# Two-layer graph attention on one Trainium2 core: twelve edge tiles of each layer read row by row from SyncE, with the rows' places in registers

## The chip, the core and the metric

The kernel runs on one core of a Trainium2 chip. The time is the device time of one execution in microseconds (us). Before the change it is 2088.41 us, the median of 3 runs (2086.89 to 2090.06).

## What is computed

The reference normalises `x` (6250 nodes of 768 numbers), runs two graph attention layers over 100,000 edges sorted by destination, and a small network per node, and adds the result to `x`. Cut to what matters:

```python
h = jnp.maximum(_layernorm(x, axis=-1), 0.0)
h = relu(gat_conv(h, src, dst, W1, a_src1, a_dst1, b1, heads=4))      # 256 wide
h = relu(gat_conv(h, src, dst, W2, a_src2, a_dst2, b2, heads=1))
out = x + relu(h @ Wm1 + bm1) @ Wm2 + bm2

def gat_conv(x, src, dst, W, a_src, a_dst, bias, heads):
    h = (x @ W).reshape(n, heads, -1)
    e = leaky_relu(alpha_s[src] + alpha_d[dst], 0.2)     # then a softmax over the edges of each dst
    out = segment_sum(h[src] * alpha[:, :, None], dst)
```

So each layer needs, for every edge, the row `h[src]` of a table in HBM, with a few numbers on the scores of that source beside it.

## The kernel before, in words

**Tiles.** 128 edges make a tile; 782 tiles hold the 100,000 edges. Two tiles make a pair (one buffer `G` of 128 x 2 rows), two pairs a group `g`, and there are 196 groups (`NG`) in each layer. 128 nodes make a node tile; there are 49 (`NT`).

**Stages.** First the features of layer 1 are computed node tile by node tile, kept in SBUF (`kept`), and written to `table[1]` (`store1`, L541). Then `layer_edges` (L688) runs over the groups for layer 1, and again for layer 2. While layer 1 runs, each finished node tile is turned into a row block of `table[2]` (`Node1.steps`, L1051 to L1079). In layer 2 each finished node tile goes through the small network to the output (`Node2.steps`, L1164).

**Gathering.** `gather(g)` (L705) reads the rows of group `g`: for each tile one indirect DMA issued by GpSimd (L722), which reads the 128 rows that 128 indices name. It is called up to 8 groups ahead of use (`AHEAD`, L945). The buffers `G` come in turn from a pool of 20 (L280). Some pairs are fetched in another way: 27 pairs of layer 1 (`SOON`) were gathered during the first stage, stored in HBM (`soon_d`), and come back by one ordinary DMA of SyncE (L324); rows that did not exist yet are filled in by matmuls with a mask (L350). Ten pairs of layer 2 (`NEXT`) are treated likewise (L380, L391). So GpSimd issues 728 tiles of layer 1 and 762 of layer 2 at L722.

**Use.** `pair(g, p)` (L791) takes a pair: VectorE forms the weights of its edges (L800 to L813), TensorE adds the weighted rows by destination (L824). `pair(g, 0)` and `pair(g, 1)` stand at two places of the loop over groups (L937 to L1005).

**SyncE.** It does no arithmetic here. It issues, in the order of the program, all ordinary DMAs: in layer 1 the loads `drow` (L679) from which VectorE makes the masks, the stores of the masks `mask_d` (L741), the `soon` loads (L324, L330), and the stores to `table[2]` (L1078); in layer 2 the loads of the masks (L686), of `x` (L1143), and the stores of the output (L1223). The DMAs take eight semaphores in turn, and each DMA waits until the one eight before it has landed, so at most eight are in flight. A DMA whose data are not made yet holds up what stands behind it on SyncE.

The numbers of a table row: 256 features, the ones for the softmax's sums, and the powers of the scores, 268 in layer 1 and 259 in layer 2 (`TW`, L176).

Of the kernel before, what the change touches and what calls it, by code (L numbers as in the profile page):

```python
# [10 lines left out]
F32 = mybir.dt.float32  # L11
BF16 = mybir.dt.bfloat16
I32 = mybir.dt.int32
AF = mybir.ActivationFunctionType
ALU = mybir.AluOpType
AX = mybir.AxisListType

P = 128
# [3 lines left out]
HID = 256  # L22
# [34 lines left out]
NEXT_GROUP = [16 * i + 11 for i in range(len(NEXT))]  # L57
NEXT_AT = {2 * g + 1: i for i, g in enumerate(NEXT_GROUP)}
NEXT_FROM = min(NEXT)


def portions(there):
# [30 lines left out]
def kernel(  # L93
# [79 lines left out]
    heads = {1: 4, 2: 1}  # L173

    RW = {1: 4 * (HID // 4 + 1), 2: HID + 2}
    TW = {1: RW[1] + 8, 2: RW[2] + 1}  # L176
    table, sd = {}, {}
    for layer, H in heads.items():
        table[layer] = dram.tile([NT * P, TW[layer]], F32, name=f"table{layer}")
# [48 lines left out]
    def powers(e1, e2, s):  # L228

        nc.scalar.activation(e1, s, AF.Exp)  # L230
        nc.scalar.activation(e2, s, AF.Exp, scale=SLOPE)
# [4 lines left out]
    def edge_places(ones):  # L236

        dst_i = ones.tile([P, NET], I32, name="dst_i")
        dri = ones.tile([NCH, CH], I32, name="dri")
        nc.sync.dma_start(src_i, src_cols)  # L240
        yield
        yield
        soonest = sorted(range(len(SOON)), key=SOON.__getitem__)
        for i in range(0, len(SOON), 2):
            for k in soonest[i:i + 2]:
                soon_places(k)
            yield
        for to, of in ((dst_i, dst_cols), (dri, dst_rows)):
            nc.sync.dma_start(to, of)
            yield  # L250
            yield
        for layer in bT:
            with nc.allow_non_contiguous_dma(reason="256 numbers"):
                nc.sync.dma_start(bT[layer], {1: b1, 2: b2}[layer].rearrange("(k p) -> p k", p=P))
            yield
        b = ones.tile([P, OUT_DIM // P], F32, name="b")
        with nc.allow_non_contiguous_dma(reason="768 numbers"):
            nc.sync.dma_start(b, bm2.rearrange("(p k) -> p k", p=P))
        yield

        drm = ones.tile([NCH, CH], BF16, name="drm")
        nc.scalar.activation(dst_f, dst_i, AF.Copy)
        yield
        for d, to in ((dst_i, dcol), (dri, drm)):
            nc.vector.tensor_scalar(d, d, PAD_DST | P - 1, None, ALU.bitwise_and)
            yield
            nc.scalar.activation(to, d, AF.Copy)
            yield
        nc.sync.dma_start(dmod_d, drm)
        bp = ones.tile([P, 3, OUT_DIM // P], BF16, name="bp")  # L270
        rest = ones.tile([P, 2, OUT_DIM // P], F32, name="brest")
        in_parts(nc.vector, [bp[:, k] for k in range(3)], b, rest[:, 0], rest[:, 1])
        yield
        with nc.allow_non_contiguous_dma(reason="768 numbers"):
            nc.sync.dma_start(bm2_d.rearrange("s (p k) -> p s k", p=P), bp)
# [1 line left out]


    bT = {layer: const.tile([P, KH], F32, name=f"bT{layer}") for layer in (1, 2)}
    gp = edges_stack.enter_context(tc.tile_pool(name="gathered", bufs=2 * (AHEAD + 2)))  # L280
    rowsp = edges_stack.enter_context(tc.tile_pool(name="rows", bufs=3))
    maskp = edges_stack.enter_context(tc.tile_pool(name="masks", bufs=6))

# [73 lines left out]
    def soon_whole(G, k):  # L357
        i, t = divmod(k, 2)
        row = G[soon_pair[i]][:, t]
        nc.vector.scalar_tensor_tensor(row, row, soon_ok[:, i, t:t + 1], soon_m.pop(k),  # L360
                                       ALU.mult, ALU.add)

    next_i = const.tile([P, len(NEXT), 2], I32, name="next_i")
    next_ok = const.tile([P, len(NEXT), 2], F32, name="next_ok")
# [80 lines left out]
    with tc.tile_pool(name="w1p", bufs=1) as wp, tc.tile_pool(name="x1", bufs=6) as xp, \  # L445
# [72 lines left out]
        def keep1(i, h_ps, rstd):  # L518
            row = kept[i]
            nc.scalar.activation(heads_row(row)[:, :, :HID // 4],  # L520
                                 h_ps[:, :HID].rearrange("p (h c) -> p h c", h=4), AF.Copy, scale=rstd)
            if i >= BARE:
                nc.scalar.activation(sd[1][:, i], h_ps[:, HID:], AF.Copy, scale=rstd)
                powers(row[:, RW[1]:RW[1] + 4], row[:, RW[1] + 4:], sd[1][:, i, :4])

        def halve(of):

# [8 lines left out]

        def scores1(i):
            nc.vector.tensor_reduce(sd[1][:, i], halves.pop(i), AX.X, ALU.add)
            powers(kept[i][:, RW[1]:RW[1] + 4], kept[i][:, RW[1] + 4:], sd[1][:, i, :4])

        def store1(i):  # L541
            nc.sync.dma_start(table[1][i * P:(i + 1) * P], kept[i])
# [1 line left out]
        halves = {}  # L544
        for row in kept:
            nc.gpsimd.memset(heads_row(row)[:, :, HID // 4:], 1.0)
        warm_ps = ps.tile([P, 4 * P], F32, name="warm_ps", tag="o", bufs=3)

        def warm(n):
# [138 lines left out]
    def layer_edges(layer, H, node, pre, matched, pre_pool):  # L688
# [4 lines left out]
        with tc.tile_pool(name=f"eg{layer}", bufs=6) as eg, \  # L693
# [11 lines left out]
            def gather(g):  # L705
                if not 0 <= g < NG:
                    return
                for t in tiles(g):
                    k = TPG * g + t
                    soon = k // 2 in (SOON_AT if layer == 1 else NEXT_AT)  # L710
                    if k // 2 not in G:
                        skip = int(g >= SHORT and k // 2 % (4 if g < SHORT + 7 else 2 if g < SHORT + 14 else 1) == 0)
                        skip += g >= SHORT + 21
                        G[k // 2] = (soon_back(SOON_AT[k // 2], skip) if soon and layer == 1 else
                                     next_back(NEXT_AT[k // 2], skip) if soon else
                                     rows_in(layer, skip))
                    if soon:
                        continue
                    n = min(P, LEAD + E - k * P)
                    if n < P:  # L720
                        nc.vector.memset(G[k // 2][:, k % 2], 0.0)
                    nc.gpsimd.indirect_dma_start(  # L722
                        out=G[k // 2][:n, k % 2], out_offset=None, in_=table[layer],
                        in_offset=bass.IndirectOffsetOnAxis(ap=src_i[:n, k:k + 1], axis=0))
# [66 lines left out]
            def pair(g, p):  # L791

                if 2 * p not in tiles(g):
                    return
                Gp = G.pop(TPG // 2 * g + p)
                e1, e2 = ((Gp[:, :, RW[1]:RW[1] + 4], Gp[:, :, RW[1] + 4:]) if layer == 1 else
                          (Gp[:, :, HID:HID + 1], Gp[:, :, HID + 2:]))
                at = TPG * (g % 4) + 2 * p
                v = w = e_ps[g // 4][:, at:at + 2]
                nc.vector.tensor_mul(v, e2, v)  # L800
                if layer == 2:
                    w = sm.tile([P, 2, H], F32, name="w")
                    nc.vector.tensor_max(w, v, e1)  # L803
                    hw = hwp.tile([P, 2, P], F32, name="hw")
                    for t in range(2):
                        k = TPG * g + 2 * p + t
                        nc.vector.tensor_scalar(hw[:, t], iota_ps, dcol[:, k:k + 1], w[:, t],  # L807
                                                ALU.is_equal, ALU.mult)
                else:
                    nc.vector.tensor_max(w, v, e1)  # L810
                    hw = hwp.tile([P, 2, H, C + 1], F32, name="hw")
                    nc.vector.tensor_mul(  # L812
                        hw, Gp[:, :, :RW[1]].rearrange("p t (h c) -> p t h c", h=H),  # L813
                        w.unsqueeze(3).to_broadcast([P, 2, H, C + 1]))
                u = g // 2
                if u not in o_ps:
                    o_ps[u] = ps.tile([P, RW[layer]], F32, name="o_ps", tag="o", bufs=3)
                for t in range(2):
                    k = 2 * p + t
                    if layer == 2:  # L820
                        l, r = hw[:, t], Gp[:, t]
                    else:
                        l, r = hot[g][:, k], hw[:, t].rearrange("p h c -> p (h c)")
                    nc.tensor.matmul(o_ps[u], l, r[:, :RW[layer]], start=(g % 2 == 0 and k == 0),  # L824
                                     stop=(g % 2 == 1 and k == tiles(g)[-1]))
# [111 lines left out]
            for g in range(NG):  # L937
# [7 lines left out]
                while gathered < min(NG, g + 1 + min(AHEAD, max(4, SHORT - g), max(2, SHORT + 19 - g))):  # L945
                    gather(gathered)
                    gathered += 1
                pair(g, 0)
                if g == NG - 1:
                    pair(g, 1)  # L950
# [42 lines left out]
                    next_steps(g, pre_pool, sm, G)  # L993
                if layer == 1 and 100 <= g < 100 + len(NEXT):
                    next_places(g - 100)
                if g < NG - 1:
                    pair(g, 1)
                advance(g, 1)
# [29 lines left out]
    with tc.tile_pool(name="w2p", bufs=1) as wp, tc.tile_pool(name="wk2", bufs=2) as wk:  # L1028
# [4 lines left out]
        class Node1:  # L1033
# [17 lines left out]
            def steps(self, t, sum_, most=None, last=None):  # L1051
# [21 lines left out]
                renewed.add(t)  # L1073
                row = kept[t][:, :TW[2]]
                nc.scalar.activation(row[:, :HID], h_ps[:, :HID], AF.Copy)
                powers(row[:, HID:HID + 1], row[:, HID + 2:], h_ps[:, HID:HID + 1])
                nc.vector.memset(row[:, HID + 1:HID + 2], 1.0)
                nc.sync.dma_start(table[2][t * P:(t + 1) * P], row)  # L1078
                nc.scalar.activation(sd[2][:, t], h_ps[:, HID:], AF.Copy)  # L1079
# [459 lines left out]
```

## Time and profile before

| what | value |
|---|---|
| median of 3 runs | 2088.41 us |
| the profiled execution's own time | 2088.15 us |
| its span in the profile | 2086.1 us |
| GpSimd (POOL) busy | 1528.1 us, 73% |
| TensorE (PE) busy | 1730.2 us, 83% |
| VectorE (DVE) busy | 1472.2 us, 71% |
| first and last indirect DMA of L722 begin at | 167.43 us, 2065.66 us |
| layer 1: first pair, and first pair of group 188, begin at | 175.56 us, 1056.02 us |
| layer 2: the same two | 1120.07 us, 2036.07 us |

A line of the profile such as `L722 POOL DMA_INDIRECT G<-table,src_i` is a group of instructions: the line of the kernel, the engine, the operation, what is written from what. `SPq` is the queue of SyncE: the time that it takes to issue a DMA is shown in the order of time, but not counted as busy. Idle time is put down to what ended it ("issue" is time in which an engine waits for nothing that the profile shows). The views used are the page (groups of instructions with their sums), the timeline, the windows (busy time of each engine in a stretch), the view of one source line, the list of DMA issues, and the chain of work that ended last.

### The profile page before, as it was taken

The page shows a single profiled execution, that of the slowest core. Times are in us where ns is not written, and L with a number is a line of the kernel's source. Part 1 is how long each engine was busy: PE and PEld are TensorE (multiplying, and loading weights), DVE is VectorE, ACT ScalarE, POOL GpSimd, SP SyncE. Part 2 cuts the span into 40 slices and gives each one's busy share as a digit, 9 for nine tenths or more (in the row PEclk, how much of TensorE's full clock was granted, in tenths as well). Part 3 has the DMA queues.
Part 4 walks back from the last instruction along what each step waited for, and adds up shares of the span by engine and source line. Part 5 has one row for each costly group of instructions (what it writes and reads, how often), then busy time and mean ns, then how long its engine had stood idle before and what let it go on. Part 6 is the DMA issues. An engine that isn't in the chain of part 4 may idle for free.

```text
span 2086.1 us, 28258 instructions
## 1 busy us (share of the span) xinstructions
PE 1730.2 (83%) x8323; PEld 1292.4 (62%) x8325; DVE 1472.2 (71%) x4315; ACT 449.3 (22%) x1409; POOL 1528.1 (73%) x1666
## 2 busy tenths in 40 slices
PE   9995989999999899888774887787787787787877
PEld 6883768778777687666542555555555555555544
DVE  7756888998989899888873655665565565565554
ACT  5761111111111121111120111111111111111111
POOL 7167777777777777777777777777777777777774
PEclk9997999999999999998996899989998998988889
DMA  9999666666666666666649466556556556555553
GB/s 346 294 336 336 183 174 186 189 191 186 178 184 191 188 184 176 188 191 184 168 124 270 125 184 191 166 181 189 169 178 189 172 174 190 171 176 181 170 178 113
DMA packets 173752, 403.78 MB, mean 194 GB/s; under 512 B 37063, under 2 KB 61470, under 8 KB 173590
## 3 DMA queue, kind: packets, MB, share of 16 engines
q0 software_dynamic: 75040, 210.90, 37.9%
q1 hardware_dynamic: 97180, 189.49, 26.0%
q10 hardware_dynamic: 1370, 1.48, 0.3%
q8 instruction: 70, 1.15, 0.2%
q14 instruction: 92, 0.75, 0.1%
HBM read 333.42 MB, written 68.31 MB: 193 GB/s over the span
## 4 chain that ended last, share of the span: by engine, by line
PE 28%; DMA 25%; DVE 22%; issue 13%; POOL 9%; DVEq 0%; ACT 0%; SPq 0%; POOLq 0%; ACTq 0%
DMA G<-table,src_i 22%; PE o_ps L824 11%; POOL G L722 8%; PE y_ps L1194 5%; DVE hw L812 5%; PE h_ps L515 4%; PE missing L350 4%; DVE hot L750 3%; DVE soon_hit L337 3%; DVE iota_ps L800 2%; DVE iota_ps L810 2%; DVE hw L807 2%; DVE mask L739 1%; DMA xt<-in_x 1%; DMA xTt<-in_xT 1%
## 5 line engine op out<-in xcount | busy, mean ns | idle before, releaser
L722 POOL DMA_INDIRECT G<-table,src_i x1490 | 1420.4, 953 | 454.0 <-issue 319.3
L824 PE MATMUL o_ps<-G,hw 128*128 128x258 f32 x1564 | 457.6, 427 | 206.5 <-DVE hw L807 204.8
L824 PE MATMUL o_ps<-hw,hot 128*128 128x260 f32 x1564 | 427.9, 412 | 112.2 <-DVE hw L812 108.6
L824 PEld LDWEIGHTS o_ps<-G,hw 128*128 128x128 f32 x1564 | 305.2, 208 | 332.9 <-DVE hw L807 273.9
L800 DVE TENSOR_TENSOR iota_ps<-G,iota_ps 128x8 f32<-128x8 f32 (+1 forms) x782 | 130.2, 166 | 442.1 <-DMA G<-table,src_i 431.4
L824 PEld LDWEIGHTS o_ps<-hw,hot 128*128 128x128 f32 x1564 | 300.3, 200 | 206.4 <-DVE hw L812 152.1
L844 ACT ACTIVATE sum<-acc 32x260 f32<-32x260 f32 (+1 forms) x384 | 160.0, 417 | 1133.5 <-DVE acc L835 1069.8
L350 PE MATMUL missing<-kept,soon_hit 128*128 128x268 f32 x1396 | 339.0, 394 | 0.0
L807 DVE TENSOR_SCALAR hw<-iota_ps,dcol,w 128x128 f32<-128x128 f32 x782 | 285.0, 406 | 14.5
L812 DVE TENSOR_TENSOR hw<-G,iota_ps 128x520 f32<-128x520 f32 x391 | 272.0, 696 | 30.2 <-DVE iota_ps L810 1.4
L350 PEld LDWEIGHTS missing<-kept,soon_hit 128*128 128x128 f32 x1396 | 263.2, 192 | 46.3
L1194 PE MATMUL y_ps<-wm,mT 128*128 128x384 f32 x392 | 189.4, 615 | 0.0
L515 PE MATMUL h_ps<-w,r 128*128 128x264 f32 (+1 forms) x588 | 137.1, 386 | 2.5 <-ACT r L505 2.5
L750 DVE TENSOR_TENSOR hot<-iota_ps,dcol 128x512 f32<-128x512 f32 x196 | 133.7, 682 | 0.0
L515 PEld LDWEIGHTS h_ps<-w,r 128*128 128x128 f32 x588 | 108.3, 191 | 22.0 <-ACT r L505 3.5
L1194 PEld LDWEIGHTS y_ps<-wm,mT 128*128 128x128 f32 x392 | 80.8, 228 | 57.3 <-issue 32.6
L337 DVE TENSOR_TENSOR soon_hit<-soon_of,iota_ps 128x768 f32<-128x768 int32 (+6 forms) x110 | 109.1, 992 | 0.2
L313 POOL DMA_INDIRECT G<-table,soon_i x54 | 51.4, 952 | 69.3 <-DVE cent L474 42.5
L835 DVE SCALAR_TENSOR_TENSOR acc<-acc,keep,o_ps 128x260 f32<-128x260 f32 (+1 forms) x192 | 91.4, 476 | 0.9 <-PE o_ps L824 0.9
L810 DVE TENSOR_TENSOR iota_ps<-iota_ps,G 128x8 f32<-128x8 f32 x391 | 68.2, 174 | 13.5 <-DVE iota_ps L800 0.2
L803 DVE TENSOR_TENSOR w<-iota_ps,G 128x2 f32<-128x2 f32 x391 | 62.5, 160 | 13.3
L1024 ACT ACTIVATE rT<-tp,bT 128x128 f32<-128x128 f32 x196 | 61.3, 364 | 32.9 <-PE tp L1018 31.4
(424 smaller groups left out, 1324.0 us busy)
## 6 DMA issues: line engine op xcount, KB each, us to landing
xt<-in_x SPq DMA_DIRECT2D x96, 384.0 KB
drow<-dmod_d SPq DMA_DIRECT2D x49, 512.0 KB
mask_d<-mask SPq DMA_DIRECT2D x97, 256.0 KB
mask<-mask_d SPq DMA_DIRECT2D x97, 256.0 KB
G<-table,src_i POOLq DMA_INDIRECT x1490
out<-y SPq DMA_DIRECT2D x48, 384.0 KB
xTt<-in_xT SPq DMA_DIRECT2D x36, 384.0 KB
soon_d<-G SPq DMA_DIRECT2D x27, 268.0 KB
```

The source lines that it names most:

```text
L337: nc.vector.tensor_tensor(soon_hit[k, part][:, :b - a], soon_of[i][:, t * P:(t + 1) * P].unsqueeze(1).to_broadcast([P, b - a, P]), nid_ps[ ...
L350: nc.tensor.matmul(soon_p[k], hit[:, T - a], kept[T], start=(T == there), stop=(T == NT - 1))
L515: nc.tensor.matmul(h_ps[:, :n], r[:, k], w1[:, k, :n], start=(k == 0), stop=(k == KI - 1))
L722: nc.gpsimd.indirect_dma_start(out=G[k // 2][:n, k % 2], out_offset=None, in_=table[layer], in_offset=bass.IndirectOffsetOnAxis(ap=src_i[: ...
L750: nc.vector.tensor_tensor(hot[g][:, T[0]:T[0] + n], iota_ps.unsqueeze(1).to_broadcast([P, n, P]), dcol[:, k:k + n].unsqueeze(2).to_broadca ...
L800: nc.vector.tensor_mul(v, e2, v)
L807: nc.vector.tensor_scalar(hw[:, t], iota_ps, dcol[:, k:k + 1], w[:, t], ALU.is_equal, ALU.mult)
L810: nc.vector.tensor_max(w, v, e1)
L812: nc.vector.tensor_mul(hw, Gp[:, :, :RW[1]].rearrange("p t (h c) -> p t h c", h=H), w.unsqueeze(3).to_broadcast([P, 2, H, C + 1]))
L824: nc.tensor.matmul(o_ps[u], l, r[:, :RW[layer]], start=(g % 2 == 0 and k == 0), stop=(g % 2 == 1 and k == tiles(g)[-1]))
L844: nc.scalar.activation(done[t][r], acc[r], AF.Copy)
L1194: nc.tensor.matmul(y_ps, mT[:, j], wm2[:, j, s * half:(s + 1) * half], start=False, stop=(j == KH - 1))
```

## The change

Six pairs of each layer, the first pairs of groups 33, 64, 95, 126, 157 and 188 (`EACH_GROUP`), are no longer gathered by GpSimd. Their 256 rows each are read by 256 DMAs of SyncE, each of one row. In the loop over groups, a new function `each_rows` stands ahead of each `pair`: in each of the 32 groups that end two ahead of the pair's own, SyncE first loads eight places from SBUF into eight registers with one instruction, then issues four row DMAs, and four more ahead of the group's second pair. For each row a register instruction multiplies the place by four (numbers to bytes). The windows of the six pairs follow on each other and overlap by one group, so that SyncE issues eight rows in every group from 0 to 186 and sixteen in five of them: 192 sets of eight, 1,536 rows, in each layer. The places (source index times row length) are worked out once by VectorE from a copy of the sources (`each_src`, six small DMAs in the first stage).

The rows of the tables become 269 and 263 numbers long (one and four unused numbers more); a memset of one number in each of the 49 `kept` tiles fills the gap of layer 1. The pool of `G` has 18 buffers in place of 20; the six pairs lie in a pool `each` of two buffers.

```diff
+EACH_GROUP = [33 + 31 * i for i in range(6)]
+EACH = len(EACH_GROUP)
+EACH_AT = {2 * g: i for i, g in enumerate(EACH_GROUP)}
+EACH_SLOTS = 32
+EACH_ROWS = 2 * P // EACH_SLOTS
...
-    TW = {1: RW[1] + 8, 2: RW[2] + 1}
+    TW = {1: RW[1] + 9, 2: RW[2] + 5}
...
-    gp = edges_stack.enter_context(tc.tile_pool(name="gathered", bufs=2 * (AHEAD + 2)))
+    gp = edges_stack.enter_context(tc.tile_pool(name="gathered", bufs=2 * (AHEAD + 1)))
...
+    def each_sources(pool):
+
+        each_src = pool.tile([2 * EACH, P], I32, name="each_src")
+        rows = src_rows.rearrange("k (t p) -> (k t) p", t=2)
+        for i, g in enumerate(EACH_GROUP):
+            nc.sync.dma_start(each_src[2 * i:2 * i + 2], rows[4 * g:4 * g + 2])
+        return each_src
+
+    def each_places(each_src):
+
+        for layer in heads:
+            nc.vector.tensor_scalar(each_at[layer], each_src, float(TW[layer]), None, ALU.mult)
+
+    def each_rows(layer, g, half):
+
+        W, n = TW[layer], EACH_ROWS
+        for i, at in enumerate(EACH_GROUP):
+            s = g - (at - 1 - EACH_SLOTS)
+            if not 0 <= s < EACH_SLOTS:
+                continue
+            if half == 0:
+                if s == 0:
+                    each_G[i] = eachp.tile([P, 2, max(TW.values())], F32, name="each_G")[:, :, :W]
+                regs = [nc.sync.alloc_register(f"each_{layer}_{i}_{s}_{j}") for j in range(n)]
+                nc.sync.load(regs, each_at[layer][2 * i + s * n // P:2 * i + s * n // P + 1, s * n % P:s * n % P + n])
+                each_regs[i] = regs
+            flat = table[layer].rearrange("n w -> (n w)").unsqueeze(0)
+            for j in range(half * (n // 2), (half + 1) * (n // 2)):
+                t, p = divmod(s * n + j, P)
+                place = nc.sync.snap(each_regs[i][j], donate=True, min_val=0, max_val=(NT * P - 1) * W)
+                nc.sync.dma_start(each_G[i][p:p + 1, t], flat[:, ds(place, W)])
...
+            nc.gpsimd.memset(row[:, RW[1] + 8:], 0.0)
...
+                    if k // 2 in EACH_AT:
+                        if k % 2 == 0:
+                            G[k // 2] = each_G[EACH_AT[k // 2]]
+                        continue
...
+                each_rows(layer, g, 0)
                 pair(g, 0)
...
+                each_rows(layer, g, 1)
                 if g < NG - 1:
                     pair(g, 1)
```

The first piece of SyncE's program shown is that of layer 1 about the store of node tile 1 (`kept_116`) to `table[2]` (`table_99`), before the change; `table_97` below is `table[1]`:

```order
L1078 DMA table_99<-kept_116 128x259
L741 DMA mask_d<-mask 128x1024
L324 DMA G<-soon_d 128x536
L679 DMA drow<-dmod_d 128x2048
L741 DMA mask_d<-mask 128x1024
```

The same place after the change, with rows that only repeat left out:

```order
L1128 DMA table_99<-kept_116 128x263
L789 DMA mask_d<-mask 128x1024
L404 REGISTER_ALU
L404 DMA each_G<-table_97 1x269
...
L331 DMA G<-soon_d 128x538
L398 TENSOR_LOAD each_at_168
L404 REGISTER_ALU
L404 DMA each_G<-table_97 1x269
...
L723 DMA drow<-dmod_d 128x2048
```

Between the two old neighbours on SyncE there now stand four or eight row DMAs, each with its register instruction, and the load of eight registers once a group.

GpSimd's program from the first stage's early gathers to the end of layer 2, before the change:

```order
L313 DMA G<-table_97,soon_i 128x268 x54
L722 DMA G<-table_97,src_i 128x268 x727
L722 DMA G<-table_97,src_i 32x268
L380 DMA G<-table_99,next_i 128x259 x20
L722 DMA G<-table_99,src_i 128x259 x128
L1152 TENSOR_LOAD bad_i
L722 DMA G<-table_99,src_i 128x259 x633
L722 DMA G<-table_99,src_i 32x259
```

And after it:

```order
L320 DMA G<-table_97,soon_i 128x269 x54
L770 DMA G<-table_97,src_i 128x269 x715
L770 DMA G<-table_97,src_i 32x269
L423 DMA G<-table_99,next_i 128x263 x20
L770 DMA G<-table_99,src_i 128x263 x128
L1202 TENSOR_LOAD bad_i
L770 DMA G<-table_99,src_i 128x263 x621
L770 DMA G<-table_99,src_i 32x263
```

Twelve indirect DMAs of each layer are gone; the order of the others is as it was.

More of the change, by code (lines that the diff above doesn't have):

```diff
@@ L240, in edge_places @@
         nc.sync.dma_start(src_i, src_cols)
+        each_src = each_sources(ones)
         yield
         yield
+        each_places(each_src)
         soonest = sorted(range(len(SOON)), key=SOON.__getitem__)
@@ L361, in soon_whole @@
                                        ALU.mult, ALU.add)
+    each_at = {layer: const.tile([2 * EACH, P], I32, name=f"each_at{layer}") for layer in heads}
+    eachp = edges_stack.enter_context(tc.tile_pool(name="each", bufs=2))
+    each_G, each_regs = {}, {}
+    def each_sources(pool):
[24 more added lines that the diff above has]
+                nc.sync.dma_start(each_G[i][p:p + 1, t], flat[:, ds(place, W)])
     next_i = const.tile([P, len(NEXT), 2], I32, name="next_i")
@@ L523, in keep1 @@
                 nc.scalar.activation(sd[1][:, i], h_ps[:, HID:], AF.Copy, scale=rstd)
-                powers(row[:, RW[1]:RW[1] + 4], row[:, RW[1] + 4:], sd[1][:, i, :4])
+                powers(row[:, RW[1]:RW[1] + 4], row[:, RW[1] + 4:RW[1] + 8], sd[1][:, i, :4])
         def halve(of):
@@ L538, in scores1 @@
             nc.vector.tensor_reduce(sd[1][:, i], halves.pop(i), AX.X, ALU.add)
-            powers(kept[i][:, RW[1]:RW[1] + 4], kept[i][:, RW[1] + 4:], sd[1][:, i, :4])
+            powers(kept[i][:, RW[1]:RW[1] + 4], kept[i][:, RW[1] + 4:RW[1] + 8], sd[1][:, i, :4])
         def store1(i):
@@ L795, in pair @@
                 Gp = G.pop(TPG // 2 * g + p)
-                e1, e2 = ((Gp[:, :, RW[1]:RW[1] + 4], Gp[:, :, RW[1] + 4:]) if layer == 1 else
-                          (Gp[:, :, HID:HID + 1], Gp[:, :, HID + 2:]))
+                e1, e2 = ((Gp[:, :, RW[1]:RW[1] + 4], Gp[:, :, RW[1] + 4:RW[1] + 8]) if layer == 1 else
+                          (Gp[:, :, HID:HID + 1], Gp[:, :, HID + 2:HID + 3]))
                 at = TPG * (g % 4) + 2 * p
@@ L1075, in steps @@
                 nc.scalar.activation(row[:, :HID], h_ps[:, :HID], AF.Copy)
-                powers(row[:, HID:HID + 1], row[:, HID + 2:], h_ps[:, HID:HID + 1])
+                powers(row[:, HID:HID + 1], row[:, HID + 2:HID + 3], h_ps[:, HID:HID + 1])
                 nc.vector.memset(row[:, HID + 1:HID + 2], 1.0)
```

## The prediction

> **What bounds the kernel now.** I read the groups of instructions first, for the engine that never rests, then windows in the middle of each layer.
>
> ```profile
> L722 POOL DMA_INDIRECT G<-table,src_i x1490 | 1420.4, 953 | 454.0 <-issue 319.3
> L800 DVE TENSOR_TENSOR iota_ps<-G,iota_ps 128x8 f32<-128x8 f32 (+1 forms) x782 | 130.2, 166 | 442.1 <-DMA G<-table,src_i 431.4
> 500.00:600.00 100.00, 96.84 (x505) 81.11 (x505) 92.72 (x227) 18.75 (x65) 75.65 (x80) 1.00 0.65 186
> 1500.00:1600.00 100.00, 80.39 (x369) 55.76 (x368) 57.28 (x202) 17.66 (x47) 75.73 (x80) 0.88 0.59 180
> ```
>
> In both layers GpSimd issues 80 indirect DMAs in 100 us (the count behind POOL's busy time, fifth of the pairs): one every 1.25 us, 0.953 us busy and 0.30 us of its own issue. The 0.30 us make 447 of its 454 us of idle time, so it hardly ever waits for a buffer, and VectorE waits 431 us for gathered rows at the first step of a pair. So GpSimd sets the pace: 728 gathers of layer 1 over 196 groups are 4.64 us a group, 762 of layer 2 are 4.86 us. The first pair of group 0 and of group 188 in each layer, in the timeline of VectorE, bear that out:
>
> ```profile
> 175.56 0.17 DVE L800 TENSOR_TENSOR iota_ps<-G,iota_ps 128x8 f32<-128x8 f32 x1 [2.03 <-DMA G<-table,src_i]
> 1056.02 0.17 DVE L800 TENSOR_TENSOR iota_ps<-G,iota_ps 128x8 f32<-128x8 f32 x1
> 1120.07 0.17 DVE L800 TENSOR_TENSOR iota_ps<-G,iota_ps 128x2 f32<-128x2 f32 x1 [19.77 <-DMA G<-table,src_i]
> 2036.07 0.17 DVE L800 TENSOR_TENSOR iota_ps<-G,iota_ps 128x2 f32<-128x2 f32 x1
> ```
>
> 880.5 us over 188 groups are 4.68 us a group, 916.0 us are 4.87.
>
> SyncE, which gets the new work, mostly waits for others to make its data:
>
> ```profile
> SPq L1223 <- DVE y L1198: 684.2, 43, 37.5
> SPq L1078 <- DVE kept L1077: 336.9, 47, 18.1
> SPq L741 <- DVE mask L739: 303.6, 62, 9.6
> ```
>
> **What goes.** Twelve gathers of each layer leave GpSimd: 12 x 1.25 = 15 us a layer, 30 us in all, if nothing else sets the pace. That is the most that the change can give: 2088 - 30 = 2058 us. The sum is made against the profiled execution's 2088.15 us (span 2086.1 us and 2 us around it), which is the median of the runs (2088.41) within 0.02%. About 0.2%, 4 us, is what a measurement can tell from no change.
>
> **What comes: 1,536 row DMAs a layer on SyncE.** The trace has no DMA of one row and no DMA with its place in a register, so the price is bounded by SyncE's other DMAs. First those at the kernel's start, then two rows of several in layer 1 and in layer 2, where SyncE comes from a wait:
>
> ```profile
> 0.78 0.42 SPq L225 DMA_DIRECT2D xt<-in_x  x1
> 1.25 0.41 SPq L456 DMA_DIRECT2D xTt<-in_xT  x1
> 1.72 0.43 SPq L225 DMA_DIRECT2D xt<-in_x  x1
> 2.19 0.43 SPq L558 DMA_DIRECT2D w<-in_W  x1
> 2.66 0.91 SPq L456 DMA_DIRECT2D xTt<-in_xT  x1
> ...
> 419.54 0.32 SPq L741 DMA_DIRECT2D mask_d<-mask  x1
> 419.91 0.42 SPq L679 DMA_DIRECT2D drow<-dmod_d  x1
> 420.38 0.46 SPq L330 DMA_DIRECT2D soon_of<-in_src_rows  x1
> ...
> 1217.20 0.34 SPq L1223 DMA_DIRECT2D out<-y  x1
> 1217.58 0.96 SPq L686 DMA_DIRECT2D mask<-mask_d  x2
> 1218.59 0.46 SPq L1143 DMA_DIRECT2D xt<-in_x  x1
> ```
>
> One straight behind another takes 0.42 us and 0.05 us between: starts 0.47 us apart (0.78, 1.25, 1.72, 2.19). Only a DMA that stood waiting takes 0.32 us (0.37 to the next). Shapes and sizes hardly matter: 384 KB, 512 KB and 128 KB all lie at 0.41 to 0.46. So a row of 1 KB, which shares no data movement with its issue, takes 0.47 us; 0.37 is the lower end.
>
> The registers: SyncE's one load of a register is in the view of its line.
>
> ```profile
> L1152 SPq TENSOR_LOAD <-bad_i x1: 787/787/787, 1219.1 to 1219.1; - x1
> L1152 SPq FUSED_REGOPS  x1: 181/181/181, 1219.9 to 1219.9; - x1
> L1152 SPq SEQ_ASSERT  x1: 33/33/33, 1220.2 to 1220.2; - x1
> ```
>
> A register step is bounded by the 0.033 us and the 0.181 us here, with a gap of 0.03 to 0.05 us. A single multiplication is nearest to the short one: 0.06 us, upper end 0.23. A row then costs 0.47 + 0.06 = 0.53 us, eight rows 4.24 us. A load of one register takes 0.787 + 0.05 = 0.84 us. Of eight by one instruction the seven others add at least nothing, and at most 0.23 us each; I price them as the short step, 7 x 0.06 = 0.42: 1.26 us, ends 0.84 and 2.45. A set of eight is 4.24 + 1.26 = 5.50 us.
>
> The Trainium skill's page "Runtime: NRT & Kernel Launch" (Instruction fetch mechanics) gives a register load about 0.2 us for each register. By that the eight are 1.6 us and a gap, 0.39 us more than mine, and the sum below 150 us higher (384 sets), 2760 us. The trace does not bear it out as a price by the register alone: the load of one took 0.787 us.
>
> SyncE's old work stays in its place between the rows:
>
> ```profile
> drow<-dmod_d SPq DMA_DIRECT2D x49, 512.0 KB
> mask_d<-mask SPq DMA_DIRECT2D x97, 256.0 KB
> mask<-mask_d SPq DMA_DIRECT2D x97, 256.0 KB
> out<-y SPq DMA_DIRECT2D x48, 384.0 KB
> G<-soon_d SPq DMA_DIRECT2D x27, 268.0 KB
> table<-kept SPq DMA_DIRECT2D x49, 129.5 KB
> soon_of<-in_src_rows SPq DMA_DIRECT2D x27, 128.0 KB
> ```
>
> Layer 1 has some 240 of these (masks 97, `drow` 45, `table` 49, the two `soon` loads 54) at about 0.44 us: 107 us. Layer 2 has about 215 (masks 97, output 48, `x` 50, 20 for `NEXT`) at 0.46: 99 us.
>
> **The sum.** The pair of group 188 needs all 192 sets of its layer. The first row stands on SyncE behind the first four mask stores, which the timeline has here:
>
> ```profile
> 182.96 3.46 SPq L741 DMA_DIRECT2D mask_d<-mask  x4
> ```
>
> In layer 1 SyncE comes to the first row at 182.96 + 3.46 = 186.4 us. It is through at 186.4 + 192 x 5.50 + 107 = 1349 us, where the pair was begun at 1056: 293 us late. In layer 2 it begins with the layer and needs 1056 + 99 = 1155 us, where the pair was reached in 916: 239 us. Behind group 188 the gathers of the next eight groups lie ready, and those groups run at the pace of VectorE and TensorE (93% and 80% busy in the windows), some 10 us shorter in all. 2088 + 293 + 239 - 10 = 2610 us. GpSimd's 30 us are then worth nothing, since it stands waiting for buffers.
>
> Who waits: at groups 33, 64, 95, 126, 157 and 188 VectorE waits for `each_G`, and behind it on VectorE everything, the masks too; between them `drow` and the mask loads come late, since they are queued behind the rows. As SyncE is late itself, its waits for VectorE (303.6, 336.9, 684.2 us above) go.
>
> The ends: with the row at 0.42 (0.37 and 0.05) and the load at 0.84 a set is 4.20 us, SyncE is through layer 1 at 1099 us, 43 late, and needs 905 in layer 2, where GpSimd's 15 us are won: 2088 + 43 - 15 - 10 = 2106. With 2.45 for the load a set is 6.69 us: 521 and 467 us late, 3066 us. With the long register step in each row too it would be 3590; one multiplication hardly takes that.
>
> **The small edits.** The 49 memsets are hidden by GpSimd's wait for `W`:
>
> ```profile
> 3.17 1.58 POOL L546 MEMSET kept<- 128x4 f32 x49
> 11.05 1.27 POOL L529 TENSOR_TENSOR ha<-w,a1b 128x512 f32<-128x512 f32 x1 [6.30 <-DMA w<-in_W]
> L350 PE MATMUL missing<-kept,soon_hit 128*128 128x268 f32 x1396 | 339.0, 394 | 0.0
> ```
>
> 49 took 1.58 us, and 6.30 us are idle; without that cover they cost 1.6. The matmuls of L350 get one column in 268: 1.3 us of 339, beside waits. Rows of 263 for 259 numbers add 1.5% to transfers whose engines are 59 to 65% busy (the share ahead of GB/s in the windows). Eighteen buffers for 20 cost nothing while VectorE waits for rows; behind a late SyncE they are full with 20 too. The six loads of sources are 6 x 0.47 = 2.8 us on SyncE in the first stage, where it has waits; 0.1% if nothing hides them. All these I take at nothing.
>
> **The rivals.** *SyncE keeps up, faster.* A row alone on its DMA engine may be issued more cheaply than a DMA of 128. The point from which it decides: to be through layer 1 by 1041 us SyncE may spend (1041 - 186 - 107) / 1536 = 0.487 us a row, the load's share of 0.105 to 0.16 included. So issue and multiplication must stay under 0.33 to 0.38 us, where the lowest rows make 0.42. Then GpSimd paces and the time is 2058. For it: SyncE's long waits. Against it: all the rows of SyncE's DMAs. The Trainium skill's page "DMA: Bandwidth & Descriptors" (Issuing engines are not separate DMA queues) speaks for this rival: the sequencer's time to start a DMA is usually small relative to the DMA. Here eight starts are 3.8 of 4.7 us a group, not small.
>
> *SyncE just keeps the old pace.* With 0.50 us a row, load included, GpSimd's gain and SyncE's loss cancel: 2088.
>
> *The landing paces, slower.* Eight DMAs may be in flight. In the chain, gathers took
>
> ```profile
> 1230.16 2.80 DMA G<-table,src_i
> 1237.67 5.42 DMA G<-table,src_i
> ```
>
> If a row lands after 2.80 us, 9.3 DMAs a group take 9.3 x 2.8 / 8 = 3.3 us, under the pace; at 5.42 us they take 6.3, and 192 sets are some 1,210 us: 2088 + 340 + 294 - 10 = 2712. That holds even with cheap issue.
>
> **The numbers.** SyncE's issue paces: 0.70, forecast 2610, its own range 2106 to 3066. The landing paces: 0.05. SyncE keeps up: 0.20, at 2058. The old pace: 0.05. The range runs from 2055, which takes in the rival, to 2950, above which I leave one in ten. Slower by over 0.2%: 0.75; within: 0.05; faster: 0.20.
>
> **What would show it.** Right: six waits of VectorE in each layer for `each_G`, at the groups named, several hundred us in sum; row DMAs of about 0.42 us on SyncE, loads of 1.2 us; SyncE without waits for VectorE; GpSimd under 80 gathers in 100 us. Wrong: 80 gathers in 100 us still, and waits of SyncE as before; a row's issue under 0.33 us would be the step that failed.

## The result and the profile after

| | median (range, runs) | ratio to before, 95% |
|---|---|---|
| before | 2088.39 us (2086.89 to 2090.06, 4) | |
| after | 2134.1 us (2132.72 to 2141.36, 4) | 1.023 [1.0218, 1.0243] |

The change makes the kernel 46 us slower, where 522 were forecast. The profiled execution of the changed kernel took 2141.36 us (span 2139.6), 7 us above its median, so its differences to before add up to 53.5 us.

The page of the changed kernel: its span, the chain that ended last by engine, and two groups.

```profile
span 2139.6 us, 37909 instructions
PE 27%; DMA 23%; DVE 20%; issue 12%; SPq 10%; POOL 6%; ACT 0%; DVEq 0%; POOLq 0%; ACTq 0%
L770 POOL DMA_INDIRECT G<-table,src_i x1466 | 1397.8, 953 | 522.5 <-issue 303.9
L344 DVE TENSOR_TENSOR soon_hit<-soon_of,iota_ps 128x768 f32<-128x768 int32 (+6 forms) x110 | 109.2, 993 | 59.0 <-DMA soon_of<-in_src_rows 58.5
```

SyncE's queue (SPq) makes 10% of the chain. GpSimd has 24 gathers less, but 522.5 us of idle time at them, 68.5 more than before. At least 0.30 us of its own issue stands ahead of every gather, some 447 us in all (the view puts down only 303.9 to issue, and other gaps of this length to events that fell into them). The 75 us beyond that are waits, at 14 gathers; before, no gap ahead of a gather was longer than 0.4 us. And VectorE waits 58.5 us for `soon_of`, an ordinary load of SyncE's.

Where the time went is in VectorE's timeline, at the same four pairs as in the prediction:

```profile
178.63 0.17 DVE L848 TENSOR_TENSOR iota_ps<-G,iota_ps 128x8 f32<-128x8 f32 x1 [4.35 <-DMA G<-table,src_i]
1126.93 0.17 DVE L848 TENSOR_TENSOR iota_ps<-each_G,iota_ps 128x8 f32<-128x8 f32 x1 [6.21 <-DMA each_G<-table]
1182.18 0.17 DVE L848 TENSOR_TENSOR iota_ps<-G,iota_ps 128x2 f32<-128x2 f32 x1 [13.79 <-DMA G<-table,src_i]
2093.20 0.17 DVE L848 TENSOR_TENSOR iota_ps<-each_G,iota_ps 128x2 f32<-128x2 f32 x1 [11.50 <-DMA each_G<-table]
```

From the first pair to the pair of group 188, layer 1 took 948.3 us (880.5 before), layer 2 took 911.0 (916.0 before). So the loss is layer 1's: +67.8 us; layer 2 gains 5.0. The rest is small: layer 1 begins 3.1 us later, and the ends of both layers and the turn between them are 12 us shorter.

A window in each layer says the same:

```profile
600.00:700.00 100.00, 83.91 (x433) 69.35 (x433) 80.16 (x205) 17.06 (x60) 66.18 (x69) 0.91 0.56 164
1500.00:1600.00 100.00, 79.42 (x374) 54.74 (x374) 58.42 (x204) 18.04 (x48) 75.63 (x80) 0.93 0.67 192
```

GpSimd issued 69 indirect DMAs in this stretch of layer 1 (80 before) and still 80 in layer 2. Layer 1 is uneven: its windows from 200 to 1100 us have between 68 and 80, and the low ones hold waits of 10 to 12 us (at 672, 824 and 982 us). The longest, 32 us, stands at the turn to layer 2.

What SyncE does in layer 1, in its timeline (a piece of row DMAs holds the register instructions, loads and waits between its first and its last DMA; a load ahead of the first is not shown):

```profile
500.10 6.35 SPq L404 DMA_DIRECT2D each_G<-table  x12
506.50 0.37 SPq L337 DMA_DIRECT2D soon_of<-in_src_rows  x1
507.03 5.47 SPq L404 DMA_DIRECT2D each_G<-table  x12
512.62 0.38 SPq L1128 DMA_DIRECT2D table<-kept  x1
513.09 0.38 SPq L789 DMA_DIRECT2D mask_d<-mask  x1
513.64 4.00 SPq L404 DMA_DIRECT2D each_G<-table  x8
517.68 0.36 SPq L723 DMA_DIRECT2D drow<-dmod_d  x1
518.56 1.42 SPq L404 DMA_DIRECT2D each_G<-table  x4
```

Between the pieces there is no pause longer than the 0.5 us ahead of the last: SyncE is full. Four rows without a load take 1.42 us from the first issue's start to the last one's end.

The prices, in the views of the two source lines (minimum, median and largest, ns):

```profile
L398 SPq TENSOR_LOAD <-each_at x384: 698/792/1567, 190.3 to 2086.8; - x192
L404 SPq ALU_OP  x3072: 32/33/52, 191.1 to 2091.2; - x192
L404 SPq MOVE each_G<-table x3072: 29/29/42, 191.2 to 2091.3; - x192
L404 SPq DMA_DIRECT2D each_G<-table x3072: 217/228/394, 191.7 to 2091.3; - x192
```

A row is 0.033 us for the multiplication, 0.029 for a move of a register, which the prediction did not have, 0.228 for the DMA, and gaps: undisturbed rows start 0.393 us apart. The load is 0.792 and a gap of 0.06. 8 x 0.393 + 0.85 = 4.00 us a set where nothing disturbs it. One of SyncE's other DMAs takes 0.36 us (median) in layer 1 and, with its gaps, puts off the next row by 0.46.

Added up from the start and end of each of SyncE's instructions, the 936.6 us between the first load of layer 1 (190.3) and the pair of group 188 (1126.9) are all taken: rows and loads with their gaps 784 us (4.08 a set, since the first row behind a load or another DMA takes a little longer), the 236 other DMAs 112, waits of rows until an older DMA has landed 27, and 13 of a pause that no view names. Behind every 128 of its instructions SyncE stands still for some 0.35 us, whatever instructions they are (the 0.5 us ahead of the last piece above hold one, between a row's multiplication and its move): 41 times in this stretch. In layer 2, between its two pairs, the same sum is 793 + 97 + 7 + 13 = 910 of 911.0 us. So SyncE has no time left in either layer: 5.04 us a group in layer 1, where the kernel before took 4.68, and 4.85 in layer 2, where it took 4.87.

The waits of VectorE, GpSimd and TensorE that are new or changed (us in total, times, longest):

```profile
DVE iota_ps L848 <- DMA G<-table,src_i: 276.7, 225, 13.8
DVE iota_ps L848 <- DMA each_G<-table: 95.7, 11, 16.4
DVE soon_hit L344 <- DMA soon_of<-in_src_rows: 58.5, 18, 7.1
POOL G L770 <- DVE iota_ps L848: 52.5, 33, 32.3
POOL G L770 <- DVE hw L860: 45.4, 52, 12.0
PE e_parts L816 <- DMA mask<-mask_d: 38.4, 16, 4.4
```

VectorE waits at eleven of the twelve pairs for `each_G`, six of them those of layer 2; at the other (820.3 us) it waits 10.3 us too, which the trace puts down to a `drow` that landed last. GpSimd waits for VectorE to give buffers back, and VectorE for SyncE.

### The profile page after: what moved, and what is told of

It is laid out like the page before. It is cut to its first block, busy times and chain, and to the rows that moved or that the text cites. A ratio compares the mean times of both kernels' runs of the same rounds, so it can differ in the third digit from the quotient of the medians.

```text
span 2139.6 us, 37909 instructions
## 1 busy us (share of the span) xinstructions
PE 1729.1 (81%) x8323; PEld 1313.8 (61%) x8325; DVE 1475.3 (69%) x4317; ACT 451.5 (21%) x1409; POOL 1507.8 (70%) x1691
## 4 chain that ended last, share of the span: by engine, by line
PE 27%; DMA 23%; DVE 20%; issue 12%; SPq 10%; POOL 6%; ACT 0%; DVEq 0%; POOLq 0%; ACTq 0%
DMA G<-table,src_i 11%; PE o_ps L872 11%; SPq L404 7%; POOL G L770 5%; PE missing L357 5%; PE h_ps L558 4%; DVE hw L860 4%; DMA soon_of<-in_src_rows 3%; PE y_ps L1244 3%; DVE hot L798 3%; SPq L398 2%; DVE soon_hit L344 2%; DVE iota_ps L848 2%; DVE iota_ps L858 2%; DVE hw L855 1%
## 5 line engine op out<-in xcount | busy, mean ns | idle before, releaser
L770 POOL DMA_INDIRECT G<-table,src_i x1466 | 1397.8, 953 | 522.5 <-issue 303.9
L872 PE MATMUL o_ps<-hw,hot 128*128 128x260 f32 x1564 | 434.0, 420 | 163.7 <-DVE hw L860 154.2
L872 PE MATMUL o_ps<-G,hw 128*128 128x258 f32 x1540 | 444.2, 426 | 126.1 <-DVE hw L855 125.5
L872 PEld LDWEIGHTS o_ps<-hw,hot 128*128 128x128 f32 x1564 | 310.1, 205 | 251.9 <-DVE hw L860 185.2
L357 PE MATMUL missing<-kept,soon_hit 128*128 128x269 f32 x1396 | 350.1, 403 | 0.0
L357 PEld LDWEIGHTS missing<-kept,soon_hit 128*128 128x128 f32 x1396 | 271.3, 198 | 51.2
L1244 PE MATMUL y_ps<-wm,mT 128*128 128x384 f32 x392 | 165.5, 548 | 0.0
L344 DVE TENSOR_TENSOR soon_hit<-soon_of,iota_ps 128x768 f32<-128x768 int32 (+6 forms) x110 | 109.2, 993 | 59.0 <-DMA soon_of<-in_src_rows 58.5
L320 POOL DMA_INDIRECT G<-table,soon_i x54 | 52.1, 965 | 70.7 <-DVE cent L517 42.1
L1244 PEld LDWEIGHTS y_ps<-wm,mT 128*128 128x128 f32 x392 | 72.0, 204 | 48.8 <-issue 22.2
L816 PE MATMUL e_parts<-win,mask 128*128 128x12 bf16 (+1 forms) x1564 | 56.9, 167 | 45.6 <-DMA mask<-mask_d 38.4
L816 PEld LDWEIGHTS <-mask 128*128 128x128 bf16 x1564 | 56.4, 98 | 59.3 <-DMA mask<-mask_d 39.8
```

The source lines that it names most:

```text
L344: nc.vector.tensor_tensor(soon_hit[k, part][:, :b - a], soon_of[i][:, t * P:(t + 1) * P].unsqueeze(1).to_broadcast([P, b - a, P]), nid_ps[ ...
L357: nc.tensor.matmul(soon_p[k], hit[:, T - a], kept[T], start=(T == there), stop=(T == NT - 1))
L770: nc.gpsimd.indirect_dma_start(out=G[k // 2][:n, k % 2], out_offset=None, in_=table[layer], in_offset=bass.IndirectOffsetOnAxis(ap=src_i[: ...
L1244: nc.tensor.matmul(y_ps, mT[:, j], wm2[:, j, s * half:(s + 1) * half], start=False, stop=(j == KH - 1))
```

## The experiments

Three groups of kernels ran, each beside the kernel before on its chip (2089.66, 2088.62 and 2089.99 us). The theories, in this order: first, **issue** (SyncE's time to issue sets layer 1 and just fits layer 2); second, **landing** (the eight DMAs in flight set it); third, **small edits** (row lengths, memsets, buffers, `each_src`); fourth, **lead** (SyncE has the time, but its deadlines are too tight: a row set ends one group ahead of its pair, and `soon_of`, `drow` and the masks queue behind rows).

### No rows at all

The small edits stay, the rows go back to GpSimd.

```diff
+        return            # first line of each_rows
-                    if k // 2 in EACH_AT:
+                    if False and k // 2 in EACH_AT:
```

> All small edits stay (rows of 269 and 263 numbers, 18 buffers, the memsets, the places), but no row is fetched by SyncE; GpSimd gathers all tiles again. Theories 1 and 2: as before the change, 2085 to 2093. Theory 3 (the small edits cost): 2115 to 2135.

Measured: 2095.81 us, ratio 1.0035 [1.0021, 1.0049], just outside what the first two theories gave. So about 7 of the 46 us (0.35%) do not come from the rows. The page:

```profile
q0 software_dynamic: 75040, 212.90, 38.8%
L771 POOL DMA_INDIRECT G<-table,src_i x1490 | 1420.3, 953 | 457.2 <-issue 308.3
```

GpSimd's gathers are as before (1420.4 us busy, 454.0 idle), and so are the layers: 883.2 and 912.9 us. Most of the difference lies ahead of layer 1, whose first pair begins at 181.2 us (175.6 before).

### Rows in one layer alone

In layer 2 only; the other kernel has the two conditions the other way round.

```diff
+            if layer == 1:
+                return
-                    if k // 2 in EACH_AT:
+                    if layer == 2 and k // 2 in EACH_AT:
```

> Rows from SyncE in layer 2 alone; layer 1 gathers all its tiles on GpSimd. Theory 1 (SyncE's issue of rows paces layer 1, and just fits in layer 2): layer 1 goes back to 4.68 us a group and layer 2 keeps its shorter chain of gathers, 15 us: 2070 to 2080. Theory 2 (the landing of rows, eight DMAs in flight, costs in both layers): layer 2 alone still loses, 2090 to 2110. Theory 3 (wider rows, two buffers less, the memsets): most of the loss stays, 2110 to 2130.

> Rows from SyncE in layer 1 alone. If the layers add up, this loses what the change loses and the 10 us that layer 2 alone gained against the small edits: 2140 to 2150. If layer 1 gives back less because layer 2's part hides it: 2125 to 2138.

Measured: in layer 2 alone 2085.67 us, ratio 0.9983 [0.9974, 0.9992]; in layer 1 alone 2147.92 us, 1.028 [1.0263, 1.0297]. Against the kernel without rows that is -10.1 and +52.1 us, in sum +42; the whole change is +38.3 against the same kernel, so the layers add up within 4 us. Layer 1 took 941.6 us with rows of its own and 882.6 without; layer 2 906.3 and 914.7. The loss is layer 1's alone. Layer 2 wins, but 8.4 of the 15 us that 12 gathers are worth, and its kernel came out slower than theory 1 had it: GpSimd does not wait there, but SyncE is full (792 + 97 us of work and 17 of pauses and waits in 906).

### Load longer or shorter

The same rows, with one load of sixteen registers every second group, or two loads of four in each.

```diff
-                regs = [... for j in range(n)]
+                if s % 2 == 0:
+                    regs = [... for j in range(2 * n)]
...
-            place = nc.sync.snap(each_regs[i][j], ...)
+            place = nc.sync.snap(each_regs[i][s % 2 * n + j], ...)
```

> One load of sixteen registers for two groups in place of two loads of eight. If a load costs 0.79 us whatever it loads, SyncE has 96 loads of 0.84 us less in each layer, 80 us. Theory 1: layer 1 gets near the pace of GpSimd, 2070 to 2095. Theory 2: the rows land no sooner, 2125 to 2140. Should a load cost by the register, nothing changes under either.

```diff
-                regs = [... for j in range(n)]
+            regs = [... for j in range(n // 2)]          # in both halves
...
-            place = nc.sync.snap(each_regs[i][j], ...)
+            place = nc.sync.snap(each_regs[i][j - half * (n // 2)], ...)
```

> Two loads of four registers for each set of eight rows, one ahead of each half: 192 loads of 0.84 us more in each layer, 161 us of SyncE's time. Theory 1: all of it shows in layer 1 and what exceeds layer 2's slack of some 40 us there: 2350 to 2420. Theory 2 (landing): 2130 to 2160, since the rows get more time to land.

Measured: sixteen 2116.86 us, ratio 1.0139 [1.0123, 1.0154]; four 2265.59 us, 1.0846 [1.0829, 1.0863]. Neither lies where a theory had put it: the expectations priced a load at 0.84 us whatever it loads, and it has a price by the register. The loads' own rows, of the kernel with sixteen:

```profile
L399 SPq TENSOR_LOAD <-each_at x192: 1160/1247/2208, 191.8 to 2047.7; - x192
```

and of the kernel with four:

```profile
L399 SPq TENSOR_LOAD <-each_at x768: 308/556/1506, 192.1 to 2213.9; - x192
```

Two loads of four cost SyncE 2 x 0.616 - 0.852 = 0.38 us a set more, 73 us a layer; layer 1 became 64.8 us longer (1013.1), layer 2 59.3 (970.3). Nearly all of the time added to SyncE shows, in layer 2 too: there SyncE had nothing to spare either. One load of sixteen saves 0.852 - 1.307 / 2 = 0.20 us a set, 38 us a layer; layer 1 became 16.8 us shorter (931.5), layer 2 11.0 (900.0). The time taken away shows only in part. The waits of the kernel with sixteen, VectorE's:

```profile
DVE iota_ps L849 <- DMA G<-table,src_i: 365.2, 299, 16.8
DVE iota_ps L849 <- DMA each_G<-table: 47.5, 7, 10.8
DVE soon_hit L344 <- DMA soon_of<-in_src_rows: 45.2, 14, 8.4
```

Those for SyncE's data are down from 154 to 93 us, those for GpSimd's up from 277 to 365. And SyncE's rows now wait longer for an older DMA (16.1 us in the changed kernel):

```profile
SPq L405 <- DMA drow<-dmod_d: 30.7, 28, 2.1
```

With the other older DMAs the rows' waits in layer 1 are 48 us, where they were 27. That takes back 21 of the 38 us, and the 17 left are what layer 1 gained. In layer 2 the gain ends at 900.0 us, about where the kernel with half of the rows on ScalarE's queue stands (902.9, below): there GpSimd is likely to pace again.

### More lead

Each pair's rows end five groups earlier (the six pairs lie at groups 38 to 193), and the sources of `soon` are loaded four groups earlier.

```diff
-EACH_GROUP = [33 + 31 * i for i in range(6)]
+EACH_LEAD = 5
+EACH_GROUP = [33 + EACH_LEAD + 31 * i for i in range(6)]
-    SOON_DOES.setdefault(max(at - 5 - len(todo), 0), [])...
+    SOON_DOES.setdefault(max(at - 9 - len(todo), 0), [])...
-        soon_of[i] = pool.tile([P, 2 * P], I32, name="soon_of", bufs=3)
+        soon_of[i] = pool.tile([P, 2 * P], I32, name="soon_of", bufs=4)
-            s = g - (at - 1 - EACH_SLOTS)
+            s = g - (at - 1 - EACH_LEAD - EACH_SLOTS)
```

> The same rows, each set five groups earlier against its pair (the pairs are those of groups 38, 69 and so on), and the sources of the early pairs loaded four groups earlier. SyncE's work is the same. Theory 1 (the sum of SyncE's issue paces): at most the late sources' share of some 20 us goes, 2110 to 2134. Theory 4 (SyncE has the time, but comes late against deadlines of two and three groups, each of its waits being paid in full): 2060 to 2090.

Measured: 2138.91 us, ratio 1.0244 [1.0229, 1.0259]: no gain, and slightly more than either theory had. The waits for `each_G` at a pair and for `soon_of` are gone, and another has come, in the waits of VectorE:

```profile
DVE iota_ps L849 <- DMA G<-table,src_i: 340.7, 283, 15.7
DVE mask L788 <- DMA drow<-dmod_d: 77.6, 32, 7.0
```

VectorE now waits at the mask for `drow`, the next load in SyncE's order, 77.6 us where it had 1.0 before the change. The deadline of `drow` itself was not moved, so by this alone the lag could be a matter of deadlines still. SyncE's time settles it: from the first load of layer 1 to the pair of group 188 its rows, loads, other DMAs, waits for landings and pauses make up all of the 921 us, so there is no spare time that a longer lead could use. Where the lag of the full queue is felt depends on the deadlines here; how long it is does not. The theory of the lead falls.

### Half of the rows on ScalarE's queue

The second four rows of a set, and a load of their four registers, are issued by ScalarE.

```diff
+            eng = (nc.sync, nc.scalar)[half]
+            at4 = s * n + half * (n // 2)
-                nc.sync.load(regs, ...)
+            eng.load(regs, ...)                           # four registers, in both halves
...
-                nc.sync.dma_start(each_G[i][p:p + 1, t], flat[:, ds(place, W)])
+                eng.dma_start(each_G[i][p:p + 1, t], flat[:, ds(place, W)])
```

> The four rows of each group's second half are issued by ScalarE's queue, with a load of four registers there; SyncE keeps the other four. ScalarE was busy 21% of the time. Theory 1 (SyncE's issue paces): SyncE loses some 2.3 us of work a group, layer 1 goes back to 4.6 us a group and both layers keep GpSimd's gain: 2060 to 2080. Theory 2 (rows land late, eight in flight): 2120 to 2140, since the number in flight is the same. ScalarE's own work may come late; above 2090 would mean that.

Measured: 2065.65 us (2064.77 to 2066.24, 4 runs), ratio 0.9893 [0.9878, 0.9908]: 23 us faster than before, 68 faster than the change. The rows are the same and land in the same buffers; only the issuing queue differs, and the load of eight has become two of four. The windows:

```profile
600.00:700.00 100.00, 92.38 (x472) 75.26 (x471) 91.03 (x248) 19.81 (x67) 75.92 (x80) 0.98 0.65 186
1500.00:1600.00 100.00, 81.36 (x383) 57.57 (x383) 59.46 (x210) 18.88 (x50) 75.78 (x80) 0.88 0.66 186
```

GpSimd issues 80 in 100 us again, in both layers, and SyncE rests between its rows, in its timeline:

```profile
506.36 0.36 SPq L791 DMA_DIRECT2D mask_d<-mask  x1
507.44 1.46 SPq L406 DMA_DIRECT2D each_G<-table  x4
510.46 0.36 SPq L337 DMA_DIRECT2D soon_of<-in_src_rows  x1
512.86 0.35 SPq L331 DMA_DIRECT2D G<-soon_d  x1
513.93 2.65 SPq L406 DMA_DIRECT2D each_G<-table  x4
516.70 0.38 SPq L1130 DMA_DIRECT2D table<-kept  x1
```

Layer 1 took 869.8 us, layer 2 902.9: 13.4 and 10.0 less than in the kernel without rows, of the 15 that a layer could win. A DMA of ScalarE's rows, by the view of its line, is issued in the same time as SyncE's:

```profile
L406 ACTq DMA_DIRECT2D each_G<-table x1536: 234/235/540, 176.8 to 2003.4; - x192
```

ScalarE pays with waits that stand ahead of its arithmetic; the first two of several in the view of waits:

```profile
ACT parts_sb L830 <- DMA each_G<-table: 113.4, 45, 5.3
ACT mT L1241 <- DMA each_G<-table: 96.2, 25, 6.3
```

These are hidden: ScalarE is busy for 20 us in 100. The Trainium skill's page "DMA: Bandwidth & Descriptors" (Issuing engines are not separate DMA queues) says that starting DMAs on several engines saves only the sequencer's time to start them. This run agrees: the issuing time that was taken off SyncE was worth the whole loss.

### The old row lengths

Rows of 268 and 259 numbers and no memsets: with the rows on SyncE, without them, and with half of them on ScalarE.

```diff
-    TW = {1: RW[1] + 9, 2: RW[2] + 5}
+    TW = {1: RW[1] + 8, 2: RW[2] + 1}
-            nc.gpsimd.memset(row[:, RW[1] + 8:], 0.0)
```

> Rows of 268 and 259 numbers as before, without the memsets; all else as the change. 268 and 259 numbers can be cut into 4 and 7 equal parts, 269 and 263 cannot be cut. If issue is what counts and does not depend on the parts: 2126 to 2134, the small edits' 6 us less. If each part costs SyncE or the DMA engines time: above 2140.

> No row from SyncE, and rows of 268 and 259 numbers without the memsets: of the small edits only the 18 buffers, the six loads of sources and the places stay. If the 6 us of the small edits come from the wider rows: 2086 to 2092. If from the buffers or the loads: 2094 to 2098.

> Half of the rows by ScalarE's queue, and rows of 268 and 259 numbers without the memsets. Theory 1, with the 5 us that the wider rows cost without any row from SyncE: 2058 to 2063. If the width costs nothing here: 2064 to 2067. If shorter rows cost more row by row: above 2068.

Measured: with the rows 2133.04 us, ratio 1.0214 [1.02, 1.0228]; without 2090.48 us, 1.0009 [1.0, 1.0018]; with ScalarE 2066.65 us, 0.9882 [0.9864, 0.9899]. Only without rows is a gain of the old lengths clear, 5.3 us: of the 7 us of the small edits about 5 are in the lengths and the memsets. With rows on one queue or on two the intervals of the two lengths overlap; a gain of a few us is neither shown nor excluded there. The page of the kernel without rows and with the old lengths:

```profile
q0 software_dynamic: 75040, 210.90, 38.4%
```

The gathers move 210.90 MB here and 212.90 MB with the long rows, and the first pair begins at 176.0 and at 181.2 us. That the first stage is longer because its transfers are is argued, not shown; what each of length and memsets does by itself was not tried.

## Why the prediction was right and wrong

**What bounds before: right.** Where SyncE is relieved (half of the rows on ScalarE), 24 gathers less are worth 23 us against before and 30 against the kernel with the small edits and no rows. The 30 of the forecast were the right bound.

**That SyncE's issue paces: right.** Time added to SyncE shows, halving its work takes the whole loss away, and lead does not set it. The signs were there: waits at all twelve pairs, GpSimd under 80 in places, and SyncE's waits for others nearly gone, in the view of SyncE's waits:

```profile
SPq L1128 <- DVE kept L1127: 27.8, 4, 12.0
SPq L404 <- DMA drow<-dmod_d: 16.1, 23, 1.6
SPq L1273 <- DVE y L1248: 14.4, 2, 14.2
```

The store of `kept` waited 336.9 us before, the output's 684.2 for `y`. The 12.0 us that one store of `kept` still waits begin at 1126.8 us, behind the last row of layer 1, and cost the rows nothing.

**The failed step: the price of a set.** The sum took 0.53 us for a row and 1.26 for a load, 5.50 a set; a row took 0.393 and a load 0.85 with its gap, 4.00 a set. Over 192 sets that is 288 us a layer, 576 in all. The lower end of the prediction, with 0.42 a row and 0.84 a load, gave 2106 us and was near the measured 2134. The premise behind it, "shapes and sizes hardly matter", fell: it was read from DMAs of many rows, and a DMA of one row was issued in 0.228 us. The prediction named this sign itself, an issue under 0.33 us. The load's price had the right form and too high a start: 0.556, 0.792 and 1.247 us for four, eight and sixteen registers, so 0.32 and 0.058 for each. The Trainium skill's page "Runtime: NRT & Kernel Launch" (Instruction fetch mechanics) has about 0.2 a register, an estimated 3.2 us for sixteen; for these loads from SBUF the runs showed 1.247.

**A missing term: what SyncE waits for.** With 4.00 us a set the prediction's own sum has SyncE through layer 1 at 186.4 + 768 + 107 = 1061 us, 5 late, and through layer 2 in 867, which is less than GpSimd needs: 2088 + 5 - 15 - 10 = 2068 us, a gain. So it is in part luck that the forecast had the right sign: a set that was priced too high covered what the sum left out. The pair of group 188 was reached at 1127, another 65 us later. They are 4 of a later start (190.3), 16 of rows and 5 of other DMAs above these prices, 27 of rows that wait until an older DMA has landed (16 of them behind `drow`), and 13 of the pauses behind every 128 instructions. The sum had the last two at nothing: it took the landing for short against the pace, and it did not know the pauses. On a queue that is full to the last they decide.

**Layer 2: wrong in sign.** 239 us late were forecast; it was 5.0 us shorter. SyncE is full there as well and VectorE waits for it at all six pairs, 53.8 us in sum, but its 4.85 us a group are no more than GpSimd's old 4.87. It has no room beyond that: 73 us of loads added cost 59, 38 taken away gave 11.

**Who waits: right places, wrong size.** Several hundred us were forecast at `each_G`; 95.7 were measured. In between, the prediction had `drow` and the mask loads late; it was `soon_of` in layer 1 (58.5) and the mask loads in layer 2 (38.4 us of TensorE's). It is one lag, seen where the next deadline lies; more lead moved it to `drow`.

**The small edits: not quite nothing.** 7 us of 2088 by themselves, about 5 of them the row lengths and memsets. With the rows on SyncE, or on two queues, the old lengths gave nothing that the runs can tell.

**The rivals.** *SyncE keeps up* was put below 0.487 us a row, load included. With the measured start and other DMAs the point is (1041 - 190 - 112) / 1536 = 0.481, and the old pace's (1056 - 190 - 112) / 1536 = 0.491; 784 / 1536 = 0.510 was measured, and 0.536 with the waits and pauses. So the kernel missed both by little. With a load of sixteen the price alone, 744 / 1536 = 0.485, lay under the old pace's point; the waits and pauses of 48 and 12 us put it above. *The landing* fell as the pace: by the trace's records of landings a row landed 1.9 us after its issue began (median), where the next eight rows take 3.1 us to issue, and with ScalarE's queue rows that landed no sooner cost nothing. What is left of it are the 27 us behind older DMAs that take longer: `drow` landed after 4.3 us.

**The best version** is the one with half of the rows on ScalarE: 2065.65 us, 0.9893 [0.9878, 0.9908].

## What to carry to other kernels

When work is moved to a queue that is idle, add up its whole time in each stage, the gaps between its instructions and the waits for its own older DMAs included: when it is nearly full these decide the sign. The time that an instruction takes off the queue is the distance to the next one's start, not its own duration: a row's DMA lasted 0.228 us, and the row with its two register instructions and the gaps cost 0.393. A price read from another form of instruction is a bound, not a value; when the threshold lies just below it, the chance of the other side is large. And when one issuing queue is the bound, a second engine's queue with time to spare can carry half of it, as ScalarE's did here, busy for 20 us in 100.

## What was not expected of the hardware

- The issue of a DMA of one row with its place in a register took 0.228 us on SyncE and 0.235 on ScalarE, where SyncE's DMAs of 128 rows took 0.32 to 0.46.
- A load of registers took 0.32 us and 0.058 us for each register (four, eight, sixteen on SyncE); one register, the only such load before, had taken 0.787, so the rule does not reach down to one.
- Each row has a move of a register besides its multiplication, 0.029 us.
- SyncE stood still for 0.34 to 0.40 us behind every 128 of its instructions, 82 times in the changed kernel, and ScalarE for some 0.31 to 0.34 when it issued rows. A row's two register instructions else stand 0.02 us apart. The cause is not shown.
